# An attention kernel of two layers: the first pairs' norms and projections placed among the last tiles of z, with pools at both ends of SBUF and a prologue ordered by hand

## The chip, the cores and the metric

The kernel runs on one core of one Trainium2 chip. The metric is the device time in microseconds of one execution; 3427.79 us is the median of three runs before the change (3427.22 to 3430.41). A core has a matrix engine (TensorE, "PE" in the profile; its weight loads are "PEld"), a vector engine (VectorE, "DVE"), an engine for activation functions (ScalarE, "ACT"), a general engine (GpSimd, "POOL") and one that issues transfers (SyncE, "SP"). Each takes its own instructions in order and waits on semaphores for the others. SBUF is the on-chip memory, PSUM the memory that PE writes to.

## What is computed

The input x has 128 rows of 256 positions and 256 channels. Two layers follow each other; each adds its result to x.

```python
# layer 0: attention over the 256 positions of each row, 8 heads of 32
m = _gn(x)                                  # group norm, 32 groups, over the whole of x
m_norm = layer_norm(m); z_norm = layer_norm(z)          # z: 256 x 256 x 128
q, k, v = m_norm @ Wq.T, m_norm @ Wk.T, m_norm @ Wv.T
b = z_norm @ Wb.T                           # one bias for each pair of positions and head
p = softmax(q k^T / sqrt(32) + b);  o = p v * sigmoid(m @ Wg.T + bg)
x = x + o @ Wo.T + bo
# layer 1: banded attention (|i - j| <= 16), 4 heads of 64, on _gn(x)
x = x + attention(_gn(x)) @ w_out.T + b_out
```

Layer 0 can't begin before two things are known: the group norm's mean and scale over all of x, and, for its softmax, the bias b from all of z. Both x and z are 33.5 MB.

## The kernel before, in words

`fast_kernel` has three stages: a prologue, layer 0 and layer 1. (A second function, `general_kernel`, runs only if a check of the values fails, and isn't touched.)

**Prologue.** Weights are loaded and folded. Then z is read in 16 tiles of 2 MB (`zt`, three buffers, loaded at L1053) and x in 8 blocks of 4 MB (`xa`, two buffers, L1117). For a tile of z, `z_front` runs 16 instructions of statistics on DVE (L1059), forms the variance (L1067), and raises it to the power -1/2 on POOL (L1068). `z_back`, which follows one tile later, turns the tile on PE in 8 groups of four transposes (L1082, to `ps_t`, three PSUM buffers), copies each group to SBUF on ACT (L1084, `zT`), and projects it (L1087, `ps_b`). After every second tile, `ps_b` is copied (L1094), turned back (L1097, `ps_k`), multiplied by the norms on DVE (L1103, `bt`), a constant is added on POOL (L1107), and one ACTIVATE of 512 elements per partition forms the exponential of the bias, `eb` (L1108). A block of x gets 16 instructions of statistics (L1119). After the last block `x_moments` and `finish_moments` combine them: a few small DVE instructions, two small matmuls (L966, L974), a power on POOL (L977), and the two tables `M0` and `R0` (L981). The last block of x follows the twelfth tile of z (`nx * 12 <= n * nga`).

**Layer 0.** A `Pair` is two rows of x. Its constructor loads it (`xt`, L1185). `centre` (L1193) and `scale` (L1196) apply M0 and R0 on POOL, `moments` takes statistics on DVE (L1206 to L1212), `root` raises to the power -1/2 and writes the norms to DRAM (`rs_d`, L1217), `fetch` reads them back in another layout (`rs_r`, L1222), `turn` transposes (L1231), copies (L1235) and multiplies by the norms (`xnT`, L1237). `project` makes q, k and the gate (L1249, L1253), `values` makes v (L1264, L1270). `scores` (L1283) and its exponential (L1290), `add_bias` (L1299 `e`, L1304 `eboth` on POOL) and `apply` (L1314 `ps_ov`, L1320 `ps_su`) are the attention itself. `residual` adds the output's bias to `xt` (L1199).

**What sets the order.** The loop over pairs is under `tc.manual_schedule()`: instructions stand on their queues as written. The prologue and the first pairs' start (`now, nxt, nn = pair(0), pair(1), pair(2)` and what follows) are outside of it: there a planner of the framework chooses. The pools of the prologue (`pre`, `pre1`, `pre_ps`) are closed before those of layer 0 (`l0`, `l0s`, `ps_mm`, `ps_s`, `ps_o`) are opened in the same place, so the first tile of layer 0, `xt` of pair 0, waits until the prologue has finished with what lay there.

Of the kernel before, what the change touches and what calls it, by code (L numbers as in the profile page):

```python
# [16 lines left out]
P = 128  # L17
# [756 lines left out]
def fast_kernel(  # L774
# [186 lines left out]
    def finish_moments(run, n, pool, psum, tag):  # L961

        ps = psum.tile([P, 512], F32, name=f"gps_{tag}", tag="mm")
        mean_p = pool.tile([P, G], F32, name=f"mean_{tag}", tag="gn_a")
        nc.vector.tensor_copy(mean_p, run[:, :, 1])
        nc.tensor.matmul(ps[:, :G], avg, mean_p, start=True, stop=True)  # L966
        mu = pool.tile([P, G], F32, name=f"mu_{tag}", tag="gn_b")
        nc.vector.tensor_copy(mu, ps[:, :G])
        d = pool.tile([P, G], F32, name=f"d_{tag}", tag="gn_c")
# [5 lines left out]
        rs = pool.tile([P, G], F32, name=f"rs_{tag}", tag="gn_d")  # L975
        nc.vector.tensor_scalar_add(rs, ps2[:, :G], 1e-5)
        nc.gpsimd.tensor_tensor(rs, rs, mhalf[:, :G], ALU.pow)  # L977
        M = const.tile([P, C], F32, name=f"M_{tag}")
# [3 lines left out]
        return M, R  # L982

    with tc.tile_pool(name="pre", bufs=2) as pre, tc.tile_pool(
        name="pre1", bufs=1
    ) as pre1, tc.tile_pool(name="pre_ps", bufs=2, space=PSUM) as pps:

        lnb_w = pre1.tile([P, KC, P], F32, name="lnb_w")
        for k in range(KC):
            nc.vector.tensor_scalar_mul(lnb_w[:, k, :], ones, lnb_c[:, k : k + 1])  # L990
        for w, dst in ((wq, qb), (wk, kb)):
            for m in range(KC):
                ps = pps.tile([P, 512], F32, name="b_ps", tag="mm")
                for k in range(KC):
                    nc.tensor.matmul(
                        ps[:, 0:1], w[:, k, m * P : (m + 1) * P], lnb_c[:, k : k + 1],
                        start=(k == 0), stop=(k == KC - 1),
                    )
                nc.vector.tensor_copy(dst[:, m : m + 1], ps[:, 0:1])
        nc.vector.tensor_scalar_mul(qb, qb, QS)  # L1000
        ps = pps.tile([P, 512], F32, name="b_ps", tag="mm")
        for k in range(KC):
            nc.tensor.matmul(ps[:, :C], lnb_w[:, k, :], wv[:, k, :], start=(k == 0), stop=(k == KC - 1))
        nc.vector.tensor_copy(vb_r, ps[:, :C])
        lzb_w = pre1.tile([P, P], F32, name="lzb_w")
        nc.vector.tensor_scalar_mul(lzb_w, ones, lzb_c)
        ps = pps.tile([P, 512], F32, name="b_ps", tag="mm")
        nc.tensor.matmul(ps[:, :H], lzb_w, wb, start=True, stop=True)
        nc.vector.tensor_copy(bz_r, ps[:, :H])

        for k in range(KC):
            nc.vector.tensor_scalar(wq[:, k, :], wq[:, k, :], lnw_c[:, k : k + 1], QS, ALU.mult, ALU.mult)
            nc.vector.tensor_scalar_mul(wk[:, k, :], wk[:, k, :], lnw_c[:, k : k + 1])
            nc.vector.tensor_scalar_mul(wv[:, k, :], wv[:, k, :], lnw_c[:, k : k + 1])
            nc.vector.tensor_scalar_mul(w_in[:, k, 0:C], w_in[:, k, 0:C], QS1)

        for w in (wq, wk, wv):
            ps = pps.tile([P, 512], F32, name="b_ps", tag="mm")
            for k in range(KC):
                nc.tensor.matmul(ps[:, :C], avg, w[:, k, :], start=(k == 0), stop=(k == KC - 1))  # L1020
            for k in range(KC):
                nc.vector.scalar_tensor_tensor(w[:, k, :], ps[:, :C], -1.0 / KC, w[:, k, :], ALU.mult, ALU.add)
        nc.vector.tensor_scalar_mul(wb, wb, lzw_c)
        nc.vector.tensor_scalar_mul(bin_c[:, 0:KC], bin_c[:, 0:KC], QS1)

        nc.vector.tensor_scalar_mul(bg_c, bg_c, 0.5)
        nc.vector.tensor_scalar_mul(wo.rearrange("p k n -> p (k n)"), wo.rearrange("p k n -> p (k n)"), 0.5)


        ps = pps.tile([P, 512], F32, name="b_ps", tag="mm")  # L1030
        nc.tensor.matmul(ps[:, :H], avg, wb, start=True, stop=True)
        nc.vector.tensor_sub(wb, wb, ps[:, :H])

        nga = S // GA
        st0 = pre1.tile([P, nga, G, 3], F32, name="st0")
# [5 lines left out]
        IB, IS = 32, 64  # L1041
        zjobs = [(b, i) for b in range(NB) for i in range(0, I, IB)]
        z_rows = z.rearrange("(u t) (p b) c -> t p u (b c)", t=NB, b=NB)
        wbz = pre1.tile([P, 4, 4, H], F32, name="wbz")
        nc.vector.memset(wbz, 0.0)
        for j in range(4):
            nc.vector.tensor_copy(wbz[:, j, j, :], wb)

        def z_front(b, i0):

            nonlocal zrs
            zt = pre.tile([P, IB, CZ], F32, name="zt", tag="zt", bufs=3)
            nc.sync.dma_start(  # L1053
                zt.rearrange("p (u b) c -> p u (b c)", b=NB), z_rows[b, :, i0 // NB : (i0 + IB) // NB, :]
            )

            st = pre.tile([P, IB, 3], F32, name="zst", tag="zst")
            for i in range(0, IB, 2):
                nc.vector.bn_stats(  # L1059
                    st[:, i : i + 2, :].rearrange("p i f -> p (i f)"),  # L1060
                    zt[:, i : i + 2, :].rearrange("p i c -> p c i"),
                )
            at = i0 % IS
            if at == 0:
                zrs = pre.tile([P, IS], F32, name="zrs", tag="zrs", bufs=3)
            rs = zrs[:, at : at + IB]
            nc.vector.tensor_scalar(rs, st[:, :, 2], 1.0 / CZ, 1e-5, ALU.mult, ALU.add)  # L1067
            nc.gpsimd.tensor_tensor(rs, rs, mhalf[:, :IB], ALU.pow)  # L1068
            return zt, zrs

        def z_back(b, i0, zt, rs):
            nonlocal ps_b
            at = i0 % IS
            if at == 0:
                ps_b = pps.tile([P, 512], F32, name="ps_b", tag="bias", bufs=1)
            for j in range(at // 16, (at + IB) // 16):
                zTs = []
                for g in range(4):
                    ps_t = pps.tile([P, 512], F32, name="ps_t", tag="zT", bufs=3)
                    i = (4 * j + g) * 4 - at  # L1080
                    for a in range(4):
                        nc.tensor.transpose(ps_t[:, a * P : (a + 1) * P], zt[:, i + a, :], ident)  # L1082
                    zT = pre.tile([P, 512], F32, name="zT", tag="zT", bufs=10)
                    nc.scalar.copy(zT, ps_t)  # L1084
                    zTs.append(zT)
                for g in range(4):
                    nc.tensor.matmul(  # L1087
                        ps_b[32 * g : 32 * (g + 1), :], wbz[:, j].rearrange("p a h -> p (a h)"), zTs[g],
                        start=(j == 0), stop=(j == 3),
                    )  # L1090
            if at + IB < IS:
                return
            bT = pre.tile([P, 512], F32, name="bT", tag="bT")
            nc.scalar.copy(bT, ps_b)  # L1094
            ps_k = pps.tile([P, 4, 4, 4, H], F32, name="ps_k", tag="keys", bufs=1)
            for a in range(4):
                nc.tensor.transpose(  # L1097
                    ps_k[:, a].rearrange("p g j h -> p (g j h)"), bT[:, a * P : (a + 1) * P], ident
                )
            bt = pre.tile([P, IS, H], F32, name="bt", tag="bt")  # L1100
            for j in range(4):
                q = slice(j * 16, (j + 1) * 16)
                nc.vector.tensor_tensor(  # L1103
                    bt[:, q, :].rearrange("p (g a) h -> p g a h", g=4), ps_k[:, :, :, j, :].rearrange("p a g h -> p g a h"),
                    bcast(rs[:, q].rearrange("p (g a) -> p g a", g=4), 3, H), ALU.mult,
                )
            nc.gpsimd.tensor_tensor(bt, bt, bcast(bz_r, 1, IS), ALU.add)  # L1107
            nc.scalar.activation(  # L1108
                eb[:, :, :, b * P + (i0 - at) // NB : b * P + (i0 - at + IS) // NB],
                bt.rearrange("p (u b) h -> p h b u", b=NB), AF.Exp,  # L1110
            )

        zrs = ps_b = None

        def x_block(j):
            xa = pre.tile([P, GA * NB, C], F32, name="xa", tag="xa")
            nc.sync.dma_start(xa, x[j * GA : (j + 1) * GA].rearrange("s i c -> (s i) c").rearrange("(p n) c -> p n c", p=P))  # L1117
            for g in range(0, G, 2):
                nc.vector.bn_stats(st0[:, j, g : g + 2, :].rearrange("p g f -> p (g f)"), group_pairs(xa, g))  # L1119

        def x_moments():

            each = GA * NB * GE
# [12 lines left out]
        for n, job in enumerate(zjobs):  # L1136
            front = z_front(*job)
            if behind is not None:
                z_back(*behind)
# [697 lines left out]
```

## Time and profile before

| | us |
|---|---|
| median of 3 runs | 3427.79 |
| the profiled execution | 3428.99 |
| its span | 3427.2 |
| PE busy in the span | 3259.6 (95%) |
| DVE, ACT, POOL busy | 2019.3, 1452.8, 1983.0 |
| first scores of layer 0 (L1283) start | 295.50 |

The profile shows one execution. A row of a timeline gives the start in us from the span's start, the length, the engine, the line of the kernel, the operation, the names of output and inputs with their shapes, how many instructions are merged in the row, and in brackets how long the engine stood idle before it and what released it. A row of the groups gives the sum of busy time and the mean of one instruction in ns, then the idle time before the group. "PE 16 transposes" and the like count machine instructions: an f32 matmul can be two of them.

### The profile page before, as it was taken

What the parts mean: (1) busy time and instruction counts of PE and PEld (TensorE: products, weight loads), DVE (VectorE), ACT (ScalarE), POOL (GpSimd) and SP (SyncE); (2) the same over time, 40 slices, a digit from 0 to 9 for tenths busy, and PEclk for the clock granted to TensorE, in tenths of its full rate; (3) what the DMA queues carried; (4) which work ended last, traced back from release to release, by engine and by line L of the source; (5) the groups of instructions that cost most, each with busy time, mean ns of one, the idle gap of its engine ahead of it and who ended that gap; (6) DMA issues with size and microseconds to landing.
All of it is one profiled execution on the core that took longest, in us unless ns stands there. A gap on an engine that the chain in (4) does not pass through costs nothing. (4 is left out here: it accounts for less than half of the span.)

```text
span 3427.2 us, 81116 instructions
## 1 busy us (share of the span) xinstructions
PE 3259.6 (95%) x35158; PEld 2046.7 (60%) x35158; DVE 2019.3 (59%) x3218; ACT 1452.8 (42%) x2065; POOL 1983.0 (58%) x1385
## 2 busy tenths in 40 slices
PE   5666999999999999999999999799999999999998
PEld 3333555555555555555555555467677776767776
DVE  6863566666666666666666666366644434444455
ACT  2333444444444444444444444244444444444443
POOL 3446877777877777887777775233333333333332
PEclk8877999999999999999999999899999999999999
DMA  9921122122212221222122211221212121121211
GB/s 330 393 93 47 48 72 72 54 64 67 70 45 71 72 72 48 72 72 72 48 72 72 72 48 51 73 61 52 64 52 64 52 60 55 55 61 52 64 57 52
DMA packets 198814, 262.88 MB, mean 77 GB/s; under 512 B 46289, under 2 KB 147537, under 8 KB 197297
## 3 DMA queue, kind: packets, MB, share of 16 engines
q1 hardware_dynamic: 198448, 257.61, 24.2%
q8 instruction: 278, 4.55, 0.7%
q14 instruction: 88, 0.71, 0.1%
HBM read 188.82 MB, written 68.75 MB: 75 GB/s over the span
## 5 line engine op out<-in xcount | busy, mean ns | idle before, releaser
L1304 POOL TENSOR_TENSOR eboth<-e 128x512 f32<-128x512 f32 x512 | 639.7, 1271 | 401.0 <-DVE e L1299 397.9
L1299 DVE TENSOR_TENSOR e<-ps_sc,eb 128x1024 f32<-128x1024 f32 x512 | 602.9, 1219 | 338.5 <-ACT ps_sc L1290 252.0
L1290 ACT ACTIVATE ps_sc<-ps_sc 128x1024 f32<-128x1024 f32 x512 | 492.8, 1006 | 507.4 <-PE ps_sc L1283 507.4
L1626 POOL TENSOR_TENSOR e<-e,bw 128x384 f32<-128x384 f32 x256 | 258.8, 1032 | 443.9 <-ACT e L1624 443.9
L1587 PE MATMUL ps_p<-xgT,w_in 128*128 128x512 f32 x1024 | 468.5, 600 | 0.0
L1579 POOL TENSOR_TENSOR xt<-xt,bout_r 128x1024 f32<-128x1024 f32 x64 | 151.9, 2374 | 383.1 <-PE ps_x L1576 383.1
L1679 DVE TENSOR_TENSOR yo<-ps_y,xt 128x512 f32<-128x512 f32 x128 | 88.3, 690 | 380.0 <-PE ps_y L1675 380.0
L1587 PEld LDWEIGHTS ps_p<-xgT,w_in 128*128 128x128 f32 x1024 | 188.7, 190 | 199.0 <-issue 165.9
L1283 PE MATMUL ps_sc<-qT,kT 32*128 32x256 f32 x4096 | 293.9, 400 | 1.6 <-ACT kT L1253 1.6
L1249 PE MATMUL ps_p<-xnT,wq 128*128 128x512 f32 x512 | 255.8, 622 | 20.8 <-POOL xnT L1237 20.8
L1314 PE MATMUL ps_ov<-e,v 128*32 128x256 f32 x4096 | 274.2, 385 | 0.5 <-DVE oT L1328 0.5
L1249 PE MATMUL ps_p<-xgT,wg 128*128 128x512 f32 x512 | 254.0, 618 | 0.0
L1675 PE MATMUL ps_y<-w_out,oT 128*128 128x256 f32 x1024 | 250.0, 387 | 2.6 <-DVE oT L1660 2.6
L1356 PE MATMUL ps_y<-wo,oT 128*128 128x256 f32 x1024 | 245.1, 383 | 7.2 <-POOL oT L1346 7.2
L1356 PEld LDWEIGHTS ps_y<-wo,oT 128*128 128x128 f32 x1024 | 196.5, 192 | 88.5 <-issue 59.7
L1264 PE MATMUL ps_v<-wv,xnT 128*128 128x256 f32 x1024 | 242.1, 379 | 0.0
L1283 PEld LDWEIGHTS ps_sc<-qT,kT 32*128 32x128 f32 x4096 | 185.5, 184 | 93.8 <-issue 70.5
L1249 PE MATMUL ps_p<-xnT,wk 128*128 128x512 f32 x512 | 241.1, 593 | 0.0
L1602 PE MATMUL ps_v<-w_in,xgT 128*128 128x256 f32 x1024 | 231.9, 379 | 0.0
L1657 DVE RECIPROCAL rv<-odd 128x256 f32<-128x256 f32 x128 | 224.4, 1753 | 4.4
L1602 PEld LDWEIGHTS ps_v<-w_in,xgT 128*128 128x128 f32 x1024 | 194.6, 190 | 53.3 <-issue 30.1
L1264 PEld LDWEIGHTS ps_v<-wv,xnT 128*128 128x128 f32 x1024 | 189.8, 190 | 50.8 <-issue 31.1
(164 smaller groups left out, 5022.0 us busy)
## 6 DMA issues: line engine op xcount, KB each, us to landing
zt<-in_z_dram SPq DMA_DIRECT2D x16, 2048.0 KB
xa<-in_x_dram SPq DMA_DIRECT2D x8, 4096.0 KB
xt<-in_x_dram SPq DMA_DIRECT2D x64, 512.0 KB
rvb<-rsum SPq DMA_DIRECT2D x256, 128.0 KB
x<-xo SPq DMA_DIRECT2D x16, 2048.0 KB
xt<-x SPq DMA_DIRECT2D x64, 512.0 KB
out_dram<-yo SPq DMA_DIRECT2D x63, 512.0 KB
rs_r<-rs_d SPq DMA_DIRECT2D x64, 256.0 KB
```

Of the source, the lines that this page charges most:

```text
L1249: nc.tensor.matmul(ps, w[:, k, m * P : (m + 1) * P], getattr(self, src)[:, k, :], start=(k == 0), stop=(k == KC - 1),)
L1264: nc.tensor.matmul(self.ps_v[:, b * C : (b + 1) * C], self.xnT[:, k, t * P : (t + 1) * P], wv[:, k, :], start=(k == 0), stop=(k == KC - 1),)
L1283: nc.tensor.matmul(self.pss[q // 2][:, q % 2, b, :], self.kT[rs, c, r * I + b * P : r * I + (b + 1) * P], self.qT[rs, c, r * I : (r + 1) * I],
L1290: nc.scalar.activation(self.pss[a], self.pss[a], AF.Exp)
L1299: nc.vector.tensor_tensor(e, pss[a], eb[:, h : h + 2], ALU.mult)
L1304: nc.gpsimd.tensor_tensor(t, es[a][:, :, 0, :], es[a][:, :, 1, :], ALU.add)
L1314: nc.tensor.matmul(ov[q * D0 : (q + 1) * D0, :], self.v[:, r, b, h * D0 : (h + 1) * D0], es[q // 2][:, q % 2, b, :], start=(b == 0), stop= ...
L1356: nc.tensor.matmul(self.ps_y[:, b * C : (b + 1) * C], self.oT[r][:, k, b * P : (b + 1) * P], wo[:, k, :], start=(k == 0), stop=(k == KC - 1),)
L1587: nc.tensor.matmul(ps, w_in[:, k, n * C + m * P : n * C + (m + 1) * P], self.xgT[:, k, :], start=(k == 0), stop=(k == KC - 1),)
L1602: nc.tensor.matmul(ps[:, b * C : (b + 1) * C], self.xgT[:, k, t * P : (t + 1) * P], w_in[:, k, 2 * C : 3 * C], start=(k == 0), stop=(k == ...
L1626: nc.gpsimd.tensor_tensor(e[:, q], e[:, q], bcast(bw.rearrange("p b w -> p (b w)"), 1, KC), ALU.mult)
L1675: nc.tensor.matmul(ps[:, b * C : (b + 1) * C], self.oT[r][:, k, b * P : (b + 1) * P], w_out[:, k, :], start=(k == 0), stop=(k == KC - 1),)
```

## The change

The prologue's pools are now allocated by hand: `pre_z` at the right end of SBUF, `pre_x` at the left end, and `ps_mm` in PSUM, which layer 0 goes on using. When the last block of x has been read, `pre_x` is released, and a pool for the early tiles of layer 0 (`la`: xt, xg, xgT, xnT, qT, kT, v and the small ones) is opened in its place while z goes on at the right end; the late ones (`lb`) follow there after z. New pools wait by tile (`reuse_waits="tile"`).

The whole prologue is under `tc.manual_schedule()`. The last block of x follows the ninth tile of z (`nx * 9`). From then on a generator, `starts`, is advanced twice for each tile of z, once in the middle of its statistics and once after `z_back` of the tile before; its steps are the moments, the loads of the first three pairs, pair 0's centre, scale, moments, root, fetch, turn, and its first q and k. Pair 1 is centred, scaled and measured after the last tile. The two `residual` of pairs 0 and 1 move into the loop's first pass. The constant of the bias is no longer added on POOL but given to ACT as the bias operand, for which the one ACTIVATE of 512 elements becomes eight of 64, one for each head. `lst`, `lmv` and `lrs` have two buffers instead of four.

```diff
-    def finish_moments(run, n, pool, psum, tag):
+    def moments_steps(run, n, pool, psum, tag):
...
         nc.tensor.matmul(ps[:, :G], avg, mean_p, start=True, stop=True)
+        yield
...
         nc.tensor.matmul(ps2[:, :G], avg, d, start=True, stop=True)
+        yield
...
         nc.gpsimd.tensor_tensor(rs, rs, mhalf[:, :G], ALU.pow)
+        yield
...
-        return M, R
+        yield M, R
-    with tc.tile_pool(name="pre", bufs=2) as pre, tc.tile_pool(
-        name="pre1", bufs=1
-    ) as pre1, tc.tile_pool(name="pre_ps", bufs=2, space=PSUM) as pps:
+    pz = tc.alloc_tile_pool(name="pre_z", bufs=1, side="right")
+    px = tc.alloc_tile_pool(name="pre_x", bufs=1, side="left")
+    ps_mm = tc.alloc_tile_pool(name="ps_mm", bufs=2, space=PSUM)
+    pps = tc.alloc_tile_pool(name="pre_ps", bufs=2, space=PSUM)
...
         for i in range(0, IB, 2):
+            if i == IB // 2:
+                step()
             nc.vector.bn_stats(
...
-            nc.gpsimd.tensor_tensor(bt, bt, bcast(bz_r, 1, IS), ALU.add)
-            nc.scalar.activation(
-                eb[:, :, :, b * P + (i0 - at) // NB : b * P + (i0 - at + IS) // NB],
-                bt.rearrange("p (u b) h -> p h b u", b=NB), AF.Exp,
-            )
+        for h in range(H):
+            nc.scalar.activation(
+                eb[:, h, :, b * P + (i0 - at) // NB : b * P + (i0 - at + IS) // NB],
+                bt[:, :, h].rearrange("p (u b) -> p b u", b=NB), AF.Exp, bias=bz_r[:, h : h + 1],
+            )
...
-        behind, nx = None, 0
-        for n, job in enumerate(zjobs):
-            front = z_front(*job)
-            if behind is not None:
-                z_back(*behind)
-            behind = (*job, *front)
-            if nx < nga and nx * 12 <= n * nga:
-                x_block(nx)
-                nx += 1
-                if nx == nga:
-                    M0, R0 = x_moments()
...
-                    self.st = sm.tile([P, NT, 6], F32, name="lst", tag="lst")
-                    self.mv = sm.tile([P, NT, 2], F32, name="lmv", tag="lmv")
+                self.st = la.tile([P, NT, 6], F32, name="lst", tag="lst", bufs=2)
+                self.mv = la.tile([P, NT, 2], F32, name="lmv", tag="lmv", bufs=2)
...
-        now, nxt, nn = pair(0), pair(1), pair(2)
-        for d in (now, nxt):
-            d.centre()
-            d.scale()
-            d.moments(0)
-            d.moments(1)
-            if d is now:
-                d.root()
-                d.fetch()
-            d.residual()
-        now.turn()
-        now.project("qT", 0)
-        now.project("kT", 0)
+    def starts():
+        nonlocal la, M0, R0, now, nxt, nn
+        steps = x_moments()
+        next(steps)
+        yield
+        next(steps)
+        yield
+        next(steps)
+        px.release()
+        la = tc.alloc_tile_pool(name="l0_early", bufs=1, side="left", reuse_waits="tile")
+        now = pair(0)
+        yield
+        M0, R0 = next(steps)
+        now.centre()
+        now.scale()
+        yield
+        nxt = pair(1)
+        yield
+        now.moments(0)
+        now.moments(1)
+        now.root()
+        yield
+        nn = pair(2)
+        yield
+        yield
+        now.fetch()
+        yield
+        now.turn([mm("ps_x") for _ in range(KC)])
+        yield
+        yield
+        now.project("qT", 0)
+        now.project("kT", 0)
+        yield
+
+    start = iter(())
+
+    def step():
+        next(start, None)
+
+    behind, nx = None, 0
+    with tc.manual_schedule():
+        for n, job in enumerate(zjobs):
+            front = z_front(*job)
+            if behind is not None:
+                z_back(*behind)
+            behind = (*job, *front)
+            if nx < nga and nx * 9 <= n * nga:
+                x_block(nx)
+                nx += 1
+                if nx == nga:
+                    start = starts()
+            step()
+        z_back(*behind)
+        for _ in start:
+            pass
+        for f in ("centre", "scale"):
+            getattr(nxt, f)()
+        for r in range(2):
+            nxt.moments(r)
+    pps.release()
+    pz.release()
+    lb = tc.alloc_tile_pool(name="l0_late", bufs=1, side="right", reuse_waits="tile")
...
             nn.centre()
+            if p == 0:
+                nxt.residual()
...
             nn.scale()
+            if p == 0:
+                now.residual()
```

## The prediction, written before the result was known

> **What bounds the kernel now.** I read the page's slices first (TensorE, "PE", is busy 90% or more from the fourth slice of 86 us to the last but for one), then the stage table of the beginning, then each queue's timeline there. The chain that ended last has no piece in the first 330 us, so the prologue is read from the stages.
>
> The stage table (stretch, length, busy us and instruction count of PE, PE's weight loads, DVE, ACT and POOL, then granted clock, DMA share, GB/s):
>
> ```profile
> 31.00:178.00 147.00, 94.55 (x513) 53.72 (x512) 120.28 (x289) 50.78 (x91) 60.49 (x15) 0.80 1.03 384
> 178.00:240.00 62.00, 46.00 (x270) 25.40 (x267) 48.37 (x140) 24.21 (x45) 32.75 (x7) 0.86 0.31 102
> 240.00:256.00 16.00, 3.52 (x8) 1.08 (x8) 2.52 (x10) 2.60 (x4) 8.93 (x4) 0.57 0.00 0
> 256.00:295.00 39.00, 7.92 (x16) 3.83 (x16) 5.51 (x18) 3.06 (x5) 18.42 (x10) 0.52 0.21 68
> 295.00:322.00 27.00, 25.72 (x208) 14.17 (x212) 13.80 (x22) 13.56 (x18) 19.36 (x14) 1.00 0.00 1
> ```
>
> To 178 us the transfers set the pace (share 1.03, 384 GB/s). From 178 to 256 the last tiles of z go through. From 256 to 295 nothing is full: PE works 7.9 of 39 us. From 295 PE is full, and stays so. A microsecond taken from before that start is a microsecond of the whole, as long as layer 0 then runs as it did.
>
> The 39 us are one chain, in the timelines of SP's queue, POOL and PE (start, length, line):
>
> ```profile
> 257.12 1.70 SPq L1185 DMA_DIRECT2D xt<-in_x_dram  x3
> 273.96 3.80 SPq L1217 DMA_DIRECT2D rs_d<-lrs  x2
> 282.40 3.71 SPq L1222 DMA_DIRECT2D rs_r<-rs_d  x2
> ```
>
> ```profile
> 261.17 2.34 POOL L1193 TENSOR_TENSOR xg<-xt,M_l 128x1024 f32<-128x1024 f32 x1 [5.18 <-DMA xt<-in_x_dram]
> 287.46 2.48 POOL L1237 TENSOR_TENSOR xnT<-xgT,rs_r 128x512 f32<-128x512 f32 x2 [10.09 <-DMA rs_r<-rs_d]
> ```
>
> ```profile
> 288.77 3.78 PE L1249 MATMUL ps_p<-xnT,wq 128*128 128x512 f32 x4 [20.82 <-POOL xnT L1237]
> 295.50 1.15 PE L1283 MATMUL ps_sc<-qT,kT 32*128 32x256 f32 x16 [0.78 <-ACT kT L1253]
> ```
>
> The first pair's load is asked for at 257.1, after the last eb; 13.5 us (273.96 to 287.46) are the round trip of its norms through DRAM; the first scores start at 295.5.
>
> **The change, part by part.**
>
> *1. x before z.* The last block of x now comes after nine tiles of z, not twelve. Up to it there land 9 x 2.10 + 8 x 4.19 = 52.4 MB, 50.3 of them after the first tile (27.4 us, when DVE starts on it): at 389 GB/s (the 20 us stretches between 40 and 120) 129.3 us, so 156.7. DVE needs 27.4 + 5.3 waiting for the first block + 9 x 5.6 + 8 x 9.65 + 4 x 1.2 = 165, the same pace. Last statistics done: 166.5, against
>
> ```profile
> 197.51 9.66 DVE L1119 BATCH_NORM_STATS2 st<-xa 128x6 f32<-128x512 f32 x16
> ```
>
> so M0 and R0 come 40 us sooner. Bandwidth between 380 and 400 moves this by 3 us each way, and I keep that.
>
> *2. The price of it on PE.* The order is now by hand: PE does the moments' two small matmuls before the transposes of the ninth tile. PE waits from 145 until those are done: 166.5 + 2.6 (moments, rows of 0.2 to 0.6) = 169.2, half a tile of DVE (2.8) in between, and 1.5 for the slow clock after the wait: 173.1. Seven more tiles follow. The ninth tile lies loaded at 146; this is where the change gives back most of the 40.
>
> *3. PE's tail, which now sets the start.* Rows:
>
> ```profile
> L1082 PE MATMUL ps_t<-ident,zt 128*128 128x128 f32 x512 | 78.7, 312 | 63.8 <-ACT zT L1084 38.0 <-DMA zt<-in_z_dram 25.8
> L1087 PE MATMUL ps_b<-zT,wbz 128*32 128x512 f32 x256 | 67.8, 699 | 4.5 <-ACT zT L1084 4.5
> L1084 ACT COPY zT<-ps_t 128x512 f32<-128x512 f32 x128 | 67.8, 594 | 92.6 <-PE ps_t L1082 92.4
> L1290 ACT ACTIVATE ps_sc<-ps_sc 128x1024 f32<-128x1024 f32 x11 | 10.6, 1007 | 8.8 <-PE ps_sc L1283 8.8
> L1108 ACT ACTIVATE eb<-bt 128x512 f32<-128x512 f32 x8 | 8.5, 1062 | 72.0 <-POOL bt L1107 72.0
> L1253 ACT ACTIVATE qT<-ps_p,qb 128x512 f32<-128x512 f32 x4 | 2.7, 687 | 26.3 <-PE ps_p L1249 26.3
> ```
>
> The means hold slow stretches; at full clock four groups are 2.0 + 1.9 us (218.75 to 222.6), so a tile is 7.8. From 173.1: 8 tiles 62.4; four times the copy of ps_b and the transposes into ps_k, 1.4 each, 5.6; the first pair's transposes 2.0 (L1231) and its q and k 3.9; and the stalls of part 4.
>
> *4. Eight exponentials for one.* L1107's add on POOL (8 x 1.26) goes; L1108's one ACTIVATE becomes eight of 64 elements with a bias. ACT now does them straight after the copy of ps_b, and all later copies of ps_t queue behind them, so PE stops after three groups. From rows: 0.587 at 512 and 1.007 at 1024 elements make 0.17 fixed and 0.82 ns an element; the bias adds 0.10 (0.687 against 0.587), the strided read up to 0.06: 0.38 each alone, about 0.30 in a row (two of 1024 take 1.93, not 2.01). Eight: 2.4 to 3.0. The Trainium skill ("ScalarE: Activation LUTs", "Rules for kernel authors") says about 0.3 us for every ACTIVATE with such a bias plus 0.83 ns an element: 2.8, against a hope that splitting costs nothing. One microsecond here counts four times or so (after tiles 10, 12, 14 and 16): 2.4 against 2.8 is 1.6 us in the sum. I take 2.8. Then a stall is the copy 0.6, ps_k 0.7, bt 1.2, exp 2.8 and handovers, less three groups: 3.2 us after tiles 10 and 14. After tile 12 it is 5.6, because bt stands on DVE behind the statistics of the thirteenth tile, whose load stands in SP's queue behind rs_d of pair 0; that waits for the root at 198.3 (centre and scale after R0 at 187, moments at 194 to 196.4, POOL's 5.4 us pow in front). Issued at 199.3, landed at 208, statistics to 213.7. Stalls: 12.0. What each moved DMA passes: xt 0 and xt 1 take 1.3 us of transfer each; rs_r, held until rs_d lands (8.4 us by the rows above), delays tiles 14 and 15, on which PE arrives later still.
>
> *5. The clock.*
>
> ```profile
> 243.85 2.40 PE L1087 MATMUL ps_b<-zT,wbz 128*32 128x512 f32 x4 [4.49 <-ACT zT L1084]
> 232.53 2.02 PE L1082 MATMUL ps_t<-ident,zt 128*128 128x128 f32 x16 [1.74 <-DMA zt<-in_z_dram]
> ```
>
> After 4.49 us idle, four matmuls took 2.40 instead of 0.95; after 1.74 idle nothing was lost. No row lies between. The Trainium skill ("TensorE: Matmul & The Clock Gate", Part 1) has the clock at half after an idle window of some 3.4 us: by that only the 5.6 us stall pays (1.5), and the two of 3.2 nothing; by the row of 4.49, all three. I count 1.5 for the first and 1.5 for one of the other two, since the window is said to run freely.
>
> PE is through with z at 173.1 + 62.4 + 5.6 + 2.0 + 3.9 + 12.0 + 3.0 = 262.0 and starts scores at once, as q and k have lain ready since 232. Before: 295.5, 33.5 later.
>
> *6. What is late next.* The last eight exponentials end at 266.0 and ACT turns to the scores only then; the first e runs 267.1 to 269.4 and frees the score banks, and the second scores start at 269.5 (q, k and v of 5.6 us fill PE until 268.8). Before 301.94: 32.4 saved. Pair 1's norms, round trip after a root near 266.7: xnT possible at 280, wanted at 285; hidden by 5 us, beyond which it costs one for one.
>
> *7. Residuals moved into the first pair.* Two L1199 of 2.35 on POOL, between eboth's. Before, POOL was idle 1.61 ahead of the second pair of eboth and about 2.0 ahead of the fourth. So eboth comes about 1.4 us late for ps_su, and xnT of pair 1 another 2.2 to 2.5 late for its q. I take 3.8 together; between 0.7 (if POOL's slack takes it) and 4.7.
>
> **Sum:** 32.4 - 3.8 = 28.6 us. From the second pair on, every queue holds the same work in the same order. The profiled execution is 3428.99 (span 3427.2), 1.2 above the median of the runs; 3428.99 - 28.6 = 3400.4, and against the median 3427.79 - 28.6 = **3399.2**.
>
> **Rivals.**
> - *The tail is cheaper.* Exponentials at 2.0 (-3.2), no clock loss at stalls (-3.0), 400 GB/s (-2.3): 37 saved, 3391. For it: DVE has over 13 us to spare before the last two bt. Against: the rows put the exponentials above 2.4.
> - *The norms' round trips hold SP.* If rs_d keeps SP until it lands, tile 13 comes 8 us later, and bt, the exponentials and PE with it; if pair 1's trip is 17 us instead of 13.5 behind it, no more is hidden (+3): 17 saved, 3411. For it: SP did wait 4.6 us for rs_d at 282.4. Against: only rs_r waits for that landing.
> - *Slower.* The tiles of the statistics (lst, lmv, lrs) go from four buffers to two, so L1212 on DVE waits for the rs_d of two pairs ago; behind it stand ps_sc's products, on which PE waits. Price: whatever rs_d is late, in each of some 62 pairs; it decides from 28.6/62 = 0.46 us a pair, and at 1 us the time is 3461. Against: pairs are 28.7 us apart (rs_d from 274.0 to 2085.1, 64 of them), so rs_d has 57 us for a landing that took 8.4.
> - *No effect:* PE's tail grows by all that is hidden, 28.6 us more of stalls than counted; 3428. A tail behind late z loads could do it, but the loads lead PE by 10 us and more.
>
> **How the numbers follow.** Likeliest, 25 to 34 saved: 0.60, own range 3393 to 3403. Cheaper tail: 0.16. Round trips: 0.19. No effect: 0.02. Slower: 0.03. The range 3388 to 3413 reaches to both neighbours' values: all of the first, most of the second, about half of the third, 0.83. A change under 0.2% (7 us) can't be told from none: faster 0.95, same 0.02, slower 0.03.
>
> **What would show it.** Right: last x statistics end near 166; PE idle from 145 to 170; stalls of 3 to 6 us on L1084's copies after tiles 10, 12, 14; first scores at 262, first e at 267; POOL late for ps_su in pair 0; rows of layer 0 and 1 as before. Wrong: exponentials far from 0.35 each, a transfer gap before 160, xnT of pair 1 released by its DMA, or a pair period over 28.7.

## The result, and the profile after

| | before | after |
|---|---|---|
| median of 4 runs, us | 3427.95 | 3406.15 |
| lowest and highest | 3427.22, 3430.41 | 3405.00, 3406.96 |
| the profiled execution (its span) | 3428.99 (3427.2) | 3405.00 (3403.3) |
| first scores of layer 0 start | 295.50 | 269.64 |
| second scores | 301.94 | 277.61 |
| first scores of pair 1 | 320.60 | 298.29 |

The ratio is 0.9935 (95% interval 0.9918 to 0.9952): faster, by 21.8 us of the medians, 24.0 of the profiled executions. The prediction was 3399.2, 7 us below the result, which lies inside its range of 3388 to 3413.

The stages of the changed kernel (same columns as before: stretch, length, busy time of PE, PEld, DVE, ACT and POOL, clock, DMA share, GB/s):

```profile
31.00:165.00 134.00, 69.42 (x388) 37.76 (x386) 126.91 (x290) 44.32 (x98) 48.88 (x9) 0.78 1.04 392
165.00:198.00 33.00, 23.51 (x131) 14.05 (x132) 24.65 (x77) 13.43 (x29) 21.91 (x6) 0.81 0.27 89
198.00:219.00 21.00, 13.22 (x84) 7.90 (x83) 0.75 (x3) 6.77 (x13) 5.43 (x1) 0.91 0.62 176
219.00:270.00 51.00, 39.48 (x216) 21.21 (x219) 23.85 (x77) 24.63 (x54) 28.77 (x8) 0.83 0.34 109
270.00:299.00 29.00, 25.96 (x196) 13.55 (x192) 19.01 (x35) 15.04 (x24) 24.55 (x16) 1.00 0.12 28
```

The stretch of 39 us in which PE worked 7.9 is gone. A smaller hole has opened in its place: from 198 to 219 DVE works 0.75 of 21 us. SP's queue, DVE and PE there:

```profile
196.91 0.37 SPq L1199 DMA_DIRECT2D rs_d<-lrs  x1
197.33 0.50 SPq L1167 DMA_DIRECT2D xt<-in_x_dram  x1
197.99 0.37 SPq L1061 DMA_DIRECT2D zt<-in_z_dram  x1
207.26 4.51 SPq L1204 DMA_DIRECT2D rs_r<-rs_d  x1
```

```profile
218.71 5.38 DVE L1069 BATCH_NORM_STATS2 zst<-zt 128x6 f32<-128x256 f32 x16 [20.22 <-DMA zt<-in_z_dram]
```

```profile
171.78 3.37 PE L1092 MATMUL ps_t<-ident,zt 128*128 128x128 f32 x16
194.18 0.66 PE L1092 MATMUL ps_t<-ident,zt 128*128 128x128 f32 x4 [3.12 <-ACT zT L1094]
218.82 2.79 PE L1092 MATMUL ps_t<-ident,zt 128*128 128x128 f32 x12 [7.10 <-DMA zt<-in_z_dram]
229.08 1.11 PE L1092 MATMUL ps_t<-ident,zt 128*128 128x128 f32 x4 [7.46 <-ACT zT L1094]
253.24 1.11 PE L1092 MATMUL ps_t<-ident,zt 128*128 128x128 f32 x4 [2.70 <-ACT zT L1094]
269.64 1.15 PE L1268 MATMUL ps_sc<-qT,kT 32*128 32x256 f32 x16
```

The thirteenth tile of z is asked for at 197.99, behind pair 0's write of its norms (`rs_d`, 2 KB in elements of 4 bytes) and the third pair's `xt`. It is there only at 218.7. PE waits 7.10 for it, and 7.46 more for the exponentials that wait for its statistics.

### The profile page after: what moved, and what is told of

The parts are those of the page before. It is cut to its first block, busy times and chain, and to the rows that moved or that the text cites. A ratio compares the mean times of both kernels' runs of the same rounds, so it can differ in the third digit from the quotient of the medians.

```text
span 3403.3 us, 81181 instructions
## 1 busy us (share of the span) xinstructions
PE 3253.1 (96%) x35158; PEld 2041.4 (60%) x35158; DVE 2027.8 (60%) x3218; ACT 1463.2 (43%) x2121; POOL 1974.5 (58%) x1377
## 5 line engine op out<-in xcount | busy, mean ns | idle before, releaser
L1289 POOL TENSOR_TENSOR eboth<-e 128x512 f32<-128x512 f32 x512 | 640.5, 1273 | 379.2 <-DVE e L1284 361.7
L1284 DVE TENSOR_TENSOR e<-ps_sc,eb 128x1024 f32<-128x1024 f32 x512 | 603.0, 1219 | 316.1 <-ACT ps_sc L1275 226.5
L1275 ACT ACTIVATE ps_sc<-ps_sc 128x1024 f32<-128x1024 f32 x512 | 492.7, 1006 | 506.6 <-PE ps_sc L1268 506.6
L1652 PEld LDWEIGHTS ps_v<-w_in,xgT 128*128 128x128 f32 x1024 | 194.4, 190 | 53.5 <-issue 30.1
```

The lines of the kernel that those rows point to most:

```text
L1275: nc.scalar.activation(self.pss[a], self.pss[a], AF.Exp)
L1284: nc.vector.tensor_tensor(e, pss[a], eb[:, h : h + 2], ALU.mult)
L1289: nc.gpsimd.tensor_tensor(t, es[a][:, :, 0, :], es[a][:, :, 1, :], ALU.add)
L1652: nc.tensor.matmul(ps[:, b * C : (b + 1) * C], self.xgT[:, k, t * P : (t + 1) * P], w_in[:, k, 2 * C : 3 * C], start=(k == 0), stop=(k == ...
```

## The experiments

Each edit is against the changed kernel. Ratios are to the kernel before on the same chip, whose medians there were 3425.0 to 3426.5, 1.5 to 3 us below that of the table above; times of different chips are compared with that in mind, and positions in the traces serve for single us.

**1. Who makes the thirteenth tile late?** First, a second write of the same norms, behind the first on SP's queue:

```diff
             nc.sync.dma_start(rs_d[self.p].rearrange("(t p) -> p t", p=P), self.rs)
+            if self.p == 0:
+                nc.sync.dma_start(rs_e.rearrange("(t p) -> p t", p=P), self.rs)
```

> The write of pair 0's norms (512 elements of 4 bytes) is sent twice, the second time to a spare place in DRAM, right behind the first on SP's queue. Theory A, the small write holds what stands behind it on the queue: the statistics of the thirteenth tile start some 8 to 10 us later than the 218.7 of the changed kernel, and the whole takes 8 to 10 us more (3413 to 3416). Theory B, that tile is late for a reason of its own (its own transfer, or HBM): start within 1 us of 218.7, whole within 1.5 us.

Measured 3404.31 in one run; the tile's statistics start at 218.12, and rs_r is issued at 205.9, not later than before. Twice the small packets (1068 under 512 B between 196 and 210, against 537) cost the tile nothing, so their number is not what is paid for. Theory A fails in this form. The numbers of theory B came, but a reason of the tile's own is ruled out by the runs that follow.

Then the write two steps and the third `xt` one step later, both behind the thirteenth tile's load:

```diff
     def root(self):
         nc.gpsimd.tensor_tensor(self.rs, self.rs, mhalf[:, :NT], ALU.pow)
+        if self.p > 0:
+            self.write()
+
+    def write(self):
         nc.sync.dma_start(rs_d[self.p].rearrange("(t p) -> p t", p=P), self.rs)
...
         now.root()
         yield
-        nn = pair(2)
         yield
+        now.write()
+        nn = pair(2)
         yield
         now.fetch()
```

> The write of pair 0's norms and pair 2's load are issued after the thirteenth tile's load instead of before it; the tile's load then waits only for its buffer (PE, at 189). Theory A: its statistics start near 199, the exponentials after tile 12 at 212 instead of 225, and the whole takes 10 to 13 us less than the changed kernel (3393 to 3396). Theory B: statistics still near 218, no gain.

Measured 3389.51 (3389.23 to 3391.63), ratio 0.9896 (0.988 to 0.9913), 15 us less than the run with two writes on the same chip. The tile's statistics start at 198.20, near the 199 of theory A; the gain is larger than its 10 to 13 us.

And pair 0's write on POOL's queue, in its old place in the program:

```diff
-            nc.sync.dma_start(rs_d[self.p].rearrange("(t p) -> p t", p=P), self.rs)
+            q = nc.gpsimd if self.p == 0 else nc.sync
+            q.dma_start(rs_d[self.p].rearrange("(t p) -> p t", p=P), self.rs)
```

> Pair 0's norms are written through POOL's own queue, all else as in the changed kernel. Theory A (what is held is the queue behind the write): the thirteenth tile's statistics start near 207 and the whole takes 8 to 11 us less. If the small write holds the transfer engines themselves, whichever queue it came by: still near 218, no gain.

Measured 3389.65 in one run. SP's queue and PE:

```profile
186.75 0.37 SPq L1061 DMA_DIRECT2D zt<-in_z_dram  x1
205.79 0.34 SPq L1205 DMA_DIRECT2D rs_r<-rs_d  x1
206.26 13.01 SPq L1061 DMA_DIRECT2D zt<-in_z_dram  x3
```

```profile
214.41 0.65 PE L1092 MATMUL ps_t<-ident,zt 128*128 128x128 f32 x4 [2.81 <-ACT zT L1094]
253.55 1.15 PE L1269 MATMUL ps_sc<-qT,kT 32*128 32x256 f32 x16
```

The tile is asked for at 186.75, 11 us sooner, because SP no longer stands waiting for the root. Neither expected time (207 or 218) allowed for that. It lands before its time, the 14.6 us of waiting at it become 2.81, and the first scores start 16.1 us sooner. But these two edits take away two things at once, SP's wait for the root and the write beside the load. The next two hold SP to the old moment with a 128 KB load into a tile that POOL has just written; nothing uses its data.

```diff
             nc.gpsimd.tensor_tensor(self.rs, self.rs, mhalf[:, :NT], ALU.pow)
+            if self.p == 0:
+                hold = la.tile([P, C], F32, name="hold")
+                nc.gpsimd.tensor_tensor(hold[:, :NT], self.rs, self.rs, ALU.mult)
+                nc.sync.dma_start(hold, x[0, 0:P, :])
```

With that and the write on POOL's queue:

> Pair 0's write of rs_d goes by POOL's queue, and SP is held until the root is there by a 128 KB load into a tile that POOL writes right after the root; so the thirteenth tile is issued at the same moment as in the changed kernel (198 to 199 us) with no small write ahead of it on its own queue. If a small write holds what is queued behind it on the same queue: the tile's stats start about 9 us after its issue, near 208, the time is 3394 to 3399. If a small write keeps the DMA engines from everybody, whichever queue it came by: the stats start near 218 again and the time is 3404 to 3407. If the whole loss of the changed kernel was SP's wait for the root: the stats start near 208, too, but in the run with the write behind the tile as well.

With that and the write behind the tile on SP's queue:

> SP is held until the root by the same small load, but pair 0's write and the third pair's x come behind the thirteenth tile's load on SP. No write is under way while the tile loads. If the write (on any queue) is what made the tile late: stats near 208, time 3394 to 3399 as without. If something else at that moment slows the tile (what the queues are busy with once SP has stood for 10 us): stats near 218, time 3404 to 3407.

| profiled execution | tile issued | statistics start | first scores | time |
|---|---|---|---|---|
| the changed kernel | 197.99 | 218.71 | 269.64 | 3405.00 |
| SP held, write on POOL's queue | 198.53 | 215.97 | 266.98 | 3402.99 |
| SP held, write behind the tile | 197.68 | 212.07 | 263.72 | 3399.90 |
| write on POOL's queue | 186.75 | 198.32 | 253.55 | 3389.65 |

Both runs were expected at 208 or at 218, and both fall between. What the transfers moved from 198 on, for the changed kernel, SP held with the write on POOL's queue, and SP held with the write behind the tile (last two columns: DMA share, GB/s):

```profile
198.00:202.00 4.00, 4.00 (x25) 2.36 (x24) 0.46 (x2) 2.08 (x4) 3.42 (x1) 0.92 0.28 49
202.00:206.00 4.00, 4.00 (x27) 2.30 (x26) 0.00 (x0) 2.05 (x4) 2.00 (x1) 1.00 0.21 33
206.00:210.00 4.00, 3.52 (x23) 1.74 (x21) 0.00 (x0) 2.50 (x5) 0.00 (x0) 1.00 0.39 45
210.00:214.00 4.00, 1.53 (x12) 1.29 (x12) 0.00 (x0) 0.14 (x1) 0.00 (x0) 1.00 1.04 356
```

```profile
198.00:202.00 4.00, 4.00 (x24) 2.73 (x23) 0.81 (x3) 2.15 (x4) 3.46 (x2) 0.82 0.84 246
202.00:206.00 4.00, 4.00 (x26) 2.13 (x24) 0.00 (x0) 2.05 (x4) 2.38 (x1) 1.00 1.03 50
206.00:210.00 4.00, 4.00 (x25) 2.13 (x24) 0.00 (x0) 2.05 (x4) 0.00 (x0) 1.00 0.68 131
```

```profile
198.00:202.00 4.00, 4.00 (x27) 2.26 (x26) 0.51 (x2) 2.22 (x5) 3.38 (x1) 1.00 0.92 282
202.00:206.00 4.00, 4.00 (x28) 2.30 (x28) 0.00 (x0) 2.22 (x5) 2.05 (x1) 1.00 1.10 353
206.00:210.00 4.00, 3.32 (x22) 1.66 (x21) 0.00 (x0) 1.70 (x4) 0.00 (x0) 1.00 0.89 52
```

In the changed kernel 0.5 MB passes in 12 us, just the `xt` between write and tile; the full rate, and with it the tile, comes only at about 210 (356 GB/s), 3 us after rs_d has landed (rs_r, which waits for that, is issued at 207). With the write on the other queue the loads run at full rate for a moment and then fall to 50 GB/s, with the DMA engines' busy share at 1.03. With the write behind the tile, the tile's bytes go through by about 207 (282 and 353 GB/s for 4 us each are 2.5 MB), and yet DVE is released only at 212.07, when rs_d too has landed (rs_r is issued at 212.30): of the tile's 16 completion signals in this trace twelve are there by 206.7, the last three come from 210.6 to 212.04.

So neither another queue nor the place behind the load kept it clear of the small write. While the write was under way, what was queued behind it or beside it moved at 33 to 131 GB/s instead of 350, or was reported late. The write in its turn took 8.7 us with little else under way (on POOL's queue), 10.3 in the changed kernel and 14.2 behind the tile. The Trainium skill ("DMA: Bandwidth & Descriptors", "Queues, rings and completion order") has a transfer's completion signal land only after every earlier write of the same DMA engine, whichever queue it came by. Here the small write was queued after the tile, so that rule alone doesn't give the 212.07. Why the loads slow down, and why the last signals are late, was not settled; nor was whether it is the pieces of 4 bytes that do it or any small write to DRAM.

The sizes: with SP held as before, the place behind the tile brings 5.9 of the 16.1 us between the changed kernel and the last row of the table (269.64 - 263.72). The other 10.2 (263.72 - 253.55) are not split: they hold the tile's later issue, as SP waits for the root, what follows from it on SP's queue, and what the write still costs the tile from behind. SP held with no write near the load was not run, so the write's share may be more than 5.9.

**2. The earlier turn.** If PE's tail set the start, turning the ninth tile before the moments' matmuls should bring one tile's 8 us (later expectations call it the eighth, counting from zero):

```diff
                 if nx == nga:
+                    z_back(*behind)
+                    behind = None
                     start = starts()
```

> The ninth tile is turned and projected ahead of the moments' two matmuls, so PE doesn't stand idle with it from 146. If PE's own tail sets the start (the prediction's step 3): 7 to 8 us less than the changed kernel (3398). If the thirteenth tile's landing sets it (theory A or B, PE waits 7.1 us for it at 218.8): within 1.5 us of the changed kernel.

Measured 3404.76 (3403.60 to 3405.86), ratio 0.994 (0.9924 to 0.9957), no gain, as expected if the thirteenth tile's landing sets the start: PE waits 5.25 for it, and its statistics start at 218.75 as before. That left open whether it pays once the tile is on time:

> Pair 0's write by POOL's queue, and the turn of the eighth tile ahead of the x moments. Theory: with the write on SP the thirteenth tile set the start, so the earlier turn bought nothing; without it PE's unbroken tail of turns from 171.7 to 253.6 sets the start, and taking one tile's turn (4 x 2.0 + 1.9, about 7 to 8 us) out of it starts the first scores at 246 to 248: 3382 to 3384. Rival: the tail is bound by ACT's copies or the stalls of the eight exponentials, or the z loads: 3387 to 3390, no gain over the write by POOL's queue alone (3389.7).

Measured 3392.95 (3390.33 to 3393.48), ratio 0.9903 (0.9887 to 0.992), and the first scores at 257.37 against 253.55 without the turn. Counted from the moments' second matmul the tail is longer, not shorter: 85.6 us (171.82 to 257.37) against 82.4 (171.20 to 253.55). PE and ACT:

```profile
194.64 1.11 PE L1092 MATMUL ps_t<-ident,zt 128*128 128x128 f32 x4 [10.48 <-ACT zT L1094]
```

```profile
191.69 2.44 ACT L1118 ACTIVATE eb<-bt,bz_r 128x64 f32<-128x64 f32 x8 [9.54 <-DVE bt L1113]
```

PE reaches the exponentials of tiles 9 and 10 a tile sooner and stands there, since bt is queued on DVE behind R_l, which needs POOL's power; DVE's place in the chain is unchanged. The theory fell; the rival had the means, the exponentials' stall, but not its size.

**3. The residuals.** The same with the two residuals in the prologue, pair 0's among z's last tiles and pair 1's behind them:

```diff
         yield
+        now.residual()
         yield
         now.project("qT", 0)
...
             nxt.moments(r)
+        nxt.residual()
...
-            if p == 0:
-                nxt.residual()
...
-            if p == 0:
-                now.residual()
```

> As the run with POOL's queue and the earlier turn, with the two residuals of pairs 0 and 1 put where POOL stands idle among z's last tiles. Theory: residuals inside the first pair cost 2 us there (the first pair took 28.65 us against 26.6 without them): 2 us less than that run. Rival: they are hidden in the first pair, and in the prologue they hold up the small roots on POOL: the same or 1 to 2 us more.

Measured 3389.14 (3388.82 to 3390.11), ratio 0.9895 (0.9879 to 0.9912). From the second scores to pair 1's first it is 18.66 us (264.10 to 282.76), as in the kernel before (301.94 to 320.60); with the residuals inside it was 20.68 (277.61 to 298.29). They cost 2.0. The other 1.8 of the 3.8 us between these two runs' medians isn't theirs: this run's prologue was 1.2 us ahead by the first scores. Without the earlier turn:

> Pair 0's write by POOL's queue and the two residuals among z's last tiles, with the turn of the eighth tile where the changed kernel has it. Theory: the earlier turn cost the run with it about 3.8 us (its first scores came at 257.4 against 253.6 without it: the ninth exponentials waited on VectorE behind the first pair's centre), and the residuals brought 2.0; so 3387 to 3388, first scores near 253.6, pair 1's first scores 26.6 us after them. Rival: the difference of the two runs was noise of single runs, or the residuals bring nothing by themselves: 3389 to 3391.

Measured 3388.68 (3387.99 to 3391.43), ratio 0.9892 (0.9875 to 0.9908), on another chip than the run with the turn, so the 0.5 us between the two say nothing. From the moments' second matmul to the first scores it takes 83.6 us (171.30 to 254.86) against 85.7 with the turn (170.42 to 256.13): the turn costs 2.1 us here, not the 3.8 of the theory, and the time falls between the two that were expected.

**4. The stalls of the exponentials.** On top of that (write on POOL's queue, residuals, no earlier turn), the eight exponentials are put one by one behind the copies of the next tile:

```diff
                 nc.scalar.copy(zT, ps_t)
+                if late:
+                    late.pop(0)()
...
         for h in range(H):
-            nc.scalar.activation(
+            late.append(lambda h=h: nc.scalar.activation(
...
         z_back(*behind)
+        while late:
+            late.pop(0)()
```

> As the run with POOL's queue and the residuals, with the eight exponentials of a pair of tiles put one by one behind the eight copies of the next tile, so that no copy waits for bt. Theory: the three stalls of 2.7 to 2.9 us in PE's tail and about 1 us of half clock behind them go, 8 to 9.5 us: first scores at 244 to 246, 3378 to 3380. Rival: the thirteenth to sixteenth tile's landings are next in line (the fourteenth's came at 217.9 for a use at 224.2, so up to 6 us are free) or ACT's copies become the pace (0.6 + 0.3 us for each group of four turns that take PE 0.75): 3381 to 3386.

Measured 3383.57 (3382.65 to 3385.24), ratio 0.9875 (0.9858 to 0.9891), 5.1 us less, where the theory had 8 to 9.5; the rival's 3381 to 3386 came, by the second of its reasons. The first scores start at 250.80. The stalls are gone, but ACT is now the pace in the tile after them:

```profile
192.68 0.41 ACT L1122 ACTIVATE eb<-bt,bz_r 128x64 f32<-128x64 f32 x1
192.99 0.57 ACT L1096 COPY zT<-ps_t 128x512 f32<-128x512 f32 x1
193.45 0.41 ACT L1122 ACTIVATE eb<-bt,bz_r 128x64 f32<-128x64 f32 x1
```

```profile
193.42 2.79 PE L1101 MATMUL ps_b<-zT,wbz 128*32 128x512 f32 x8
202.81 1.93 PE L1101 MATMUL ps_b<-zT,wbz 128*32 128x512 f32 x8
```

A copy and an exponential take 0.77 us, four of each 3.1, and the matmuls that wait for the copies end 0.86 later than where ACT only copies (2.79 against 1.93). That happens twice in each of three tiles, 5.2 us given back, and once in the ninth, 0.85 more. By an estimate from these rows, four copies first and four exponentials behind them should hide it (2.05 for four copies and 4 x 0.31, 3.3 us in a period of 2.0 + 1.9); this was not run.

**5. Which part of the change brings the gain?** No step of the first pairs among z's tiles, all behind the last:

```diff
     def step():
-        next(start, None)
+        pass
```

> The changed kernel with no step of the first pairs among z's tiles: x still comes before z's second half, but the moments, norms and projections all run behind the last tile. Theory: x's earlier place alone gains nothing; PE's tail ends near 248, and moments, x's load, centre, root, round trip, turn and projections take some 45 us behind it: first scores at 290 to 297, 3418 to 3428. Rival: x's earlier place is worth something by itself (VectorE is clear of x's statistics in the tail): first scores before 285, 3405 to 3415.

Measured 3411.97 in one run, first scores at 278.82: the theory missed by 6 us and more, and both numbers of the rival came.

```profile
237.01 0.66 PE L1107 MATMUL ps_k<-ident,bT 128*128 128x128 f32 x4 [0.68 <-ACT bT L1104]
254.44 1.97 PE L1215 MATMUL ps_x<-ident,xg 128*128 128x128 f32 x8 [10.72 <-POOL xg L1178]
278.82 1.15 PE L1268 MATMUL ps_sc<-qT,kT 32*128 32x256 f32 x16 [0.78 <-ACT kT L1238]
```

z is through PE at 237.7, not at 248 (its last transposes into ps_k), and the pair's chain behind it takes 41.1 us against 47.5 (248.0 to 295.5), though the moments are now in it: the load of `xt`, issued at 206.80 and not at 257.12, no longer waits for z's end. So 16.7 of the 25.9 us by which the first scores moved (295.50 to 269.64) come without any overlap; how they divide between x's place, the exponentials without POOL and the pools at two ends was not taken apart. The overlap as written adds 9.2 (278.82 to 269.64), and with the norms' write off SP's queue 25.3 (to 253.55).

And x's blocks over twelve tiles of z, as before the change, with the overlap kept:

```diff
-            if nx < nga and nx * 9 <= n * nga:
+            if nx < nga and nx * 12 <= n * nga:
```

> The changed kernel with x's blocks spread over twelve tiles of z, as before the change, in place of nine; the steps among z's tiles start three tiles later, so that the root, the round trip and the projections fall at or behind z's last tile. Theory: PE's waits in x's phase are less (145 us before against 173 after), but the pair's chain is no longer covered: first scores at 268 to 280, 3402 to 3415, not better than the change. Rival: PE's tail is what counts and x's place does not: first scores before 262, 3390 to 3397.

Measured 3396.45 in one run, 30.1 us under the kernel before on its chip where the change was 21.8 under it; first scores at 263.12, 6.5 us sooner. The theory missed, and the rival's number was met, though not its first scores before 262. SP, DVE and PE:

```profile
222.01 0.37 SPq L1061 DMA_DIRECT2D zt<-in_z_dram  x1
```

```profile
240.49 5.41 DVE L1069 BATCH_NORM_STATS2 zst<-zt 128x6 f32<-128x256 f32 x16 [17.01 <-DMA zt<-in_z_dram]
```

```profile
240.60 3.49 PE L1092 MATMUL ps_t<-ident,zt 128*128 128x128 f32 x16 [6.68 <-DMA zt<-in_z_dram]
263.12 1.15 PE L1268 MATMUL ps_sc<-qT,kT 32*128 32x256 f32 x16 [0.78 <-ACT kT L1238]
```

Here only z's last tile stands behind the write (issued at 220.50), 18.5 us from issue to use; PE waits 6.68 for it instead of 14.6 at the thirteenth, and its two longest waits around x's last block are 10.04 and 8.00 instead of one of 24.69. Given the write on SP's queue, x's earlier place costs more than it brings; with the write elsewhere this was not run.

The best version run is that of part 4: 3383.57, 43 us under the kernel before on its chip (ratio 0.9875, where the change has 0.9935).

## Why the prediction was right, and where it was off

The time lay in the range, and the chain of the first pair runs among z's tiles, as was said. But most of the gain is not from there: 16.7 of the 25.9 us come with no step of that chain among the tiles, and the overlap as written adds 9.2 where 25.3 were to be had, because of one small write and SP's wait for it: the prediction counted the wait and put the write's effect on the loads at nothing. The errors the other way (1.3 us at the start of the tail, 1.8 at the residuals) are small; the range held because it was wide.

*Step 1 and 2 (x before z, and its price on PE)*: right in its times. x's statistics end at 164.8 (166.5 was said), and PE turns the ninth tile from 171.78 (173.1): 1.3 to the good. That the earlier place is worth its price was taken for granted, and with the write where it is it was not: x over twelve tiles has the first scores 6.5 us sooner. (The slices that the prediction starts from have PE at 90% or more from the fifth on, not the fourth, and one later slice at 70%; nothing rests on it.)

*Step 3 (PE's tail sets the start)*: right in kind and only in part in fact: half-way through it the thirteenth tile's landing set the pace.

*Step 4 (exponentials and stalls)*: the row of eight took 2.44. The Trainium skill's price ("ScalarE: Activation LUTs", "Rules for kernel authors") made it 2.8; the 2.4 that the prediction worked out from the rows, at 0.30 each, was the better guide. The stalls after tiles 10 and 14 were 3.12 and 2.70 (3.2 was said). **The step that failed is the thirteenth tile's load in this part**: "issued at 199.3, landed at 208". It was issued at 197.99 and in use at 218.7, 20.7 us instead of 8.7. The working saw the write ahead of it in SP's queue and charged it for SP's wait on the root alone, not for what it does to transfers behind it. The stall there was 7.10 + 7.46 = 14.6, where 5.6 was said. The first scores came 7.6 us late (269.6 for 262.0): all stalls together 20.4 for 12.0, 8.4 more; the start of the tail 1.3 less; 0.5 in the clock and the handovers. With the write moved behind the load and SP held as before, the first scores start at 263.7 and the time is 3399.9: close to what was predicted, though the tile is in use only at 212.07 there too.

*Step 5 (clock)*: the order of size held; the idle window of 3.4 us, as the prediction took it, did not, since by it stalls of 3.12 and 2.70 cost nothing. After the 3.12 us stall eight matmuls took 2.77 instead of 1.93; after 2.70 the transposes took 1.11 instead of 0.66. With the write on POOL's queue stalls of 2.88 and 2.81 lost nothing and one of 2.73 lost about 1 us. The stretch behind the 3.12 in the changed kernel, and behind the 2.88 in the run with POOL's queue (third column from the right: granted clock):

```profile
195.30:198.60 3.30, 3.30 (x14) 1.31 (x9) 3.13 (x12) 0.28 (x1) 1.61 (x3) 0.50 0.10 7
```

```profile
195.30:198.60 3.30, 3.30 (x26) 1.96 (x22) 3.23 (x12) 1.52 (x4) 2.54 (x4) 1.00 0.00 0
```

What decides can be read from the traces. The granted clock changes only on a fixed grid of 3.41 us. From 40 to 3370 us of the 14 profiles, each of the 144 changes from full to half followed a grid step in which PE had been idle for 1.90 us or more, and no step with more than 1.96 was followed by full clock. Of the 3.12 us 2.39 lay in one step, of the 2.73 it was 2.34, and the 2.70 lay wholly in one; the 2.88 and the 2.81 were cut by the grid into 1.35 + 1.53 and 1.45 + 1.36.

*Step 6 (what is late next)*: the step from first to second scores was 7.97, 7.5 was said. Pair 1's xnT was released by POOL, not by its transfer, as said.

*Step 7 (residuals)*: 2.0, where 3.8 was taken; 1.8 to the good.

*The sum*: at the second scores 24.3 saved for 32.4; less the residuals 22.3 for 28.6 at pair 1. From there the 22.3 stay, pair after pair, to the end of layer 0. The profiled executions differ by 24.0, so 1.7 more came in layer 1, from no cause that was looked for; the runs of one kernel spread by as much.

*The rivals*: "the norms' round trips hold SP" had the right place (the thirteenth tile, behind rs_d) and a nearer size, 17 us saved and 3411, with the wrong means: SP didn't wait for the landing, it issued the tile's load at 197.99; the transfers behind the write were slow. Its counter-argument, that only rs_r waits for that landing, was the same mistake as in part 4. The slower case did not come: L1284's, L1289's and L1275's rows and the pair's period are as before.

## What to carry to other kernels

A write of 2 KB in pieces of 4 bytes was not small for the transfers around it: look for a place where no large load is under way until it has landed (8.4 to 14.2 us here), and keep an instruction that must wait for another engine off the queue that feeds the loads. When work is moved among other work, follow each queue it joins (here SP's) to what stands behind it, with the wait for issue and the time to landing as two terms. When a change gives less than its parts, take the parts one at a time: here most of the gain came with no overlap at all, and the overlap's own gain was more than halved (9.2 for 25.3) by one small write and SP's wait for it.

## What was not expected of the hardware

The write of 512 elements of 4 bytes took 8.7 us to land on POOL's queue with little else under way. Of two behind one another on SP's queue the second had landed at 207.4, one alone at 207.2. Loads beside it fell from 350 to about 50 GB/s.

The copy of R_l on DVE took nine times that of M_l, beside POOL's centre, and ended just behind it:

```profile
176.83 0.27 DVE L984 COPY M_l<-mu_l 128x256 f32<-128x256 f32 x1
185.08 2.44 DVE L984 COPY R_l<-rs_l 128x256 f32<-128x256 f32 x1 [7.98 <-POOL rs_l L979]
```

```profile
185.01 2.37 POOL L1175 TENSOR_TENSOR xg<-xt,M_l 128x1024 f32<-128x1024 f32 x1
```

The Trainium skill ("SBUF — State Buffer", "Who interferes with whom") has a copy on DVE, in the modes that use both of its ports, share one pair of ports with POOL: who issues first has it for the whole instruction, and the other waits. These rows agree. The statistics on DVE ran beside POOL at their usual 0.34 us each (2.74 for 8).
